# Layer 1's rows inside and behind the attention loop: other step lengths, products in three of four quarters, half steps of differential attention

## The chip, the cores and the metric

The kernel runs on one core of a Trainium2 chip. The metric is device time in microseconds. The kernel before took 1200.21 us (median of three runs, 1198.93 to 1204.29). A profile is of one execution, taken by the hardware profiler; its times are microseconds from the start of its span. Engines are PE (TensorE), DVE (VectorE), ACT (ScalarE), POOL (GpSimd) and SP (SyncE), each with its own queue of instructions.

## The reference

Two transformer blocks on x of shape (8, 512, 128), in float32. `ln` is a layer norm without weights.

```python
xn = ln(x)
x = x + attention_16_heads_causal(xn) + soft_mixture_of_8_experts(xn)      # layer 0
xn = ln(x)
x = x + differential_attention(xn) + block(xn)                             # layer 1

def differential_attention(x):          # per batch, 512 rows, one head of 128
    a1, a2 = softmax(q1 @ k1.T * s), softmax(q2 @ k2.T * s)
    out = (a1 - lam * a2) @ v
    return out / rms(out) * 0.2

def block(h):                           # attention runs over the 8 batches (axis 0), per row of 512
    h2 = h + causal_attention_over_batches(ln1(h)) @ proj.T
    z = ln2(h2)
    return h2 + top2_of_8_experts(z)    # each expert takes at most 1280 of the 8192 choices
```

The attention inside `block` couples, for one row position, the batch s with the batches 0 to s. So its work for batch s grows with n = s + 1, and it needs layer 0's result of the batches up to s only.

## The kernel before, in words

Rows lie on 128 partitions, four row blocks (`NI`) to a batch. The program has these stages.

1. Layer 0's mixture of experts (until about 276 us), with loads beside it.
2. **The attention loop.** It runs over steps e_ from -8 to 99; each has four quarters n, and `slot_ = 4 * e_ + n` numbers them, so the loop ends with slot 399. A step treats a third of one group of four heads of a batch (four groups to a batch, 12 steps to a batch). In each quarter PE makes scores for the exponential pass (`e_head`, L965), whose exponentials ACT takes (L970), and, eight steps ahead, scores for a pass that finds the row maxima (`m_head`, L932), which DVE reduces with a mask (L942). At the end of a step POOL masks the exponentials (`e_mask`, L975), and PE multiplies the masked exponentials of the step before with v (`av`, L989). Every half batch DVE makes `q2` (L952) from the maxima. After four groups, `out_x` (L1026) adds the result to `x_all`, and the batch's lead begins. Within the loop each engine's instructions keep exactly the order in which the program states them (`in_order`).
3. **The leads.** `lead(s)` is a generator that makes layer 1's rows of batch s: layer norm (`ln_stats`, `ln_apply`), transposes and qkv (L566, evacuated by DVE at L573), then products of q and k on POOL (`times`, L585) summed by DVE (`sum_q`, L609), softmax over batches, products with v on POOL (L585 again) summed by DVE (`sum_v`, L639), the projection, the second layer norm, routing (L697 to L761), and eight scatters of rows into the experts' slots in HBM, issued by POOL (L768). Each `yield k, where` says that the lead goes on after k slots at the earliest, and for `"pe"` only in quarter 1, for `"pool"` only in a quarter in which POOL is free for it. `step_leads` is called once a slot and takes each lead one yield further when its time has come; in one slot only one lead gets the `"pool"` grant. Leads also wait for each other's tiles (`after`).
4. **Behind the loop**, `diff([0..5])` computes differential attention of batches 0 to 5. It is a generator too: first qkv, then a first pair of scores, then 24 units (six batches, four row blocks), each with transposes (L161), scores two units ahead (L1138, maxima L1143, exponentials L1148, combination L1161) and the product with v (L1176); a batch's last unit normalises and adds into `x_all` (L1197). After each of its steps, six slots of `step_leads` follow, in each of which POOL is free. When the generator has ended, the slots go on alone until all leads have ended. Here the Tile framework's scheduler may reorder instructions.
5. The eight experts. Each loads its slots (`xe`, L1235) when all scatters of all leads have landed, runs two matrix products (L1263, L1270), and scatters its rows back (L1280).
6. `diff([6, 7])` with `final(b)` between its steps: load of the experts' rows, two additions on DVE (L1298), store.

PSUM tiles of tag `t` are seven in the loop and two behind it. A lead's value product tiles (`prod`) are three.

## Time and profile before

| | |
|---|---|
| runs, us | 1198.93, 1200.21, 1204.29 |
| profiled execution, us | 1204.13 |
| its span, us | 1202.4 |
| mean granted clock of PE | 0.917 |
| busy PE, DVE, ACT, POOL, us | 1017.4, 744.8, 547.9, 426.0 |
| last mask of the loop (L975) ends | 726.2 |
| last `x_all` of batch 5 (L1197) starts | 937.16 |
| first expert matmul (L1263) starts | 986.44 |

Busy times are unions over the span and not additive over engines. In the lists of single instructions the first number is the start in us from the start of the span, the second the length in us; then come engine, line, operation, output and inputs, shapes, and in brackets the idle time of the engine before it with what ended that. In the windows by stage each row is a stretch of the span with the busy time of each engine in it; the number of instructions is in parentheses. In the slices each digit is the busy share of a fortieth of the span in tenths (9 is 90% or more), PEclk the granted clock of PE in tenths.

### The profile page before, as it was taken

Reading aid. Unit: us, or ns where it says so; the run is one execution under the profiler, and the core shown is the slowest. Engines: PE = TensorE matmul, PEld = TensorE weight load, DVE = VectorE, ACT = ScalarE, POOL = GpSimd, SP = SyncE. Lnnn points to the kernel's source line nnn. Section 1 sums busy time; section 2 is a strip of 40 time slices with the busy share of each in tenths; the row PEclk is TensorE's granted clock in tenths of the full one; section 3 lists DMA queues with packets and bytes.
Section 4 is the critical chain, followed back from the end, with each engine's and each line's share of the span. In section 5 each row is a group of like instructions: output and inputs, shape, how many; then the busy total and the mean of one; then the engine's idle time right before and its main releaser. Section 6 shows DMA issues by size and latency. Waiting matters only on the chain. (4 is left out here: it accounts for less than half of the span.)

```text
span 1202.4 us, 19250 instructions
## 1 busy us (share of the span) xinstructions
PE 1017.4 (85%) x6780; PEld 642.4 (53%) x6780; DVE 744.8 (62%) x2622; ACT 547.9 (46%) x1236; POOL 426.0 (35%) x544
## 2 busy tenths in 40 slices
PE   3889989898999999999999996867685329998985
PEld 1457557675555545554555543544544217776753
DVE  6823533587577777877778857869797322222256
ACT  2455436332667656665566454444443102222244
POOL 4500000002144443546274357344444324544420
PEclk9899989997899999999899988789797559999998
DMA  8760000000000000000000004000000022112052
GB/s 232 168 191 1 1 1 1 1 1 1 1 1 2 1 2 1 2 17 4 4 18 1 1 19 140 1 19 0 16 1 10 9 53 66 49 32 73 11 159 71
DMA packets 48689, 41.51 MB, mean 35 GB/s; under 512 B 8747, under 2 KB 42838, under 8 KB 48592
## 3 DMA queue, kind: packets, MB, share of 16 engines
q1 hardware_dynamic: 43168, 33.19, 9.9%
q0 software_dynamic: 4608, 6.69, 1.8%
q8 instruction: 54, 0.88, 0.3%
q10 hardware_dynamic: 816, 0.39, 0.1%
q14 instruction: 43, 0.35, 0.1%
HBM read 21.88 MB, written 21.27 MB: 36 GB/s over the span
## 5 line engine op out<-in xcount | busy, mean ns | idle before, releaser
L942 DVE CUSTOM_DVE_ANT_0 junk<-sm,cmask 128x128 f32<-128x128 f32 (+3 forms) x512 | 227.8, 486 | 87.9 <-PE sm L932 50.2
L970 ACT ACTIVATE pt<-se 128x384 f32<-128x384 f32 (+1 forms) x384 | 183.6, 527 | 147.0 <-PE se L965 94.7
L932 PE MATMUL sm<-kj,qT 32*128 32x128 f32 (+3 forms) x1024 | 234.4, 497 | 7.5 <-DVE mcol L942 4.4
L965 PE MATMUL se<-q,kj 32*128 32x512 f32 (+3 forms) x1024 | 211.8, 483 | 3.8 <-DVE mcol L942 2.6
L975 POOL TENSOR_SCALAR_AFFINE_SELECT pt<-pt 128x512 f32<-128x512 f32 (+1 forms) x96 | 79.1, 824 | 189.1 <-ACT pt L970 188.9
L965 PEld LDWEIGHTS se<-q,kj 32*128 32x128 f32 x1024 | 100.7, 190 | 84.7 <-DVE mcol L942 31.4
L932 PEld LDWEIGHTS sm<-kj,qT 32*128 32x128 f32 x1024 | 113.7, 195 | 22.3 <-DVE mcol L942 9.5
L1280 POOL DMA_INDIRECT yd<-es,to x80 | 77.8, 972 | 99.2 <-DVE es L1276 78.4
L989 PE MATMUL po<-pt,vpad 128*9 128x512 f32 (+3 forms) x1024 | 89.5, 446 | 6.4 <-POOL pt L975 6.4
L1266 ACT ACTIVATE hTm<-phm 128x1024 f32<-128x1024 f32 (+1 forms) x48 | 42.2, 882 | 114.9 <-PE phm L1263 73.4
L1270 PEld LDWEIGHTS pem<-w,hTm 128*128 128x128 f32 x640 | 77.1, 191 | 17.8 <-ACT hTm L1266 11.4
L768 POOL DMA_INDIRECT xs<-l_z,sput x64 | 63.3, 988 | 57.1 <-issue 43.3
L1138 PE MATMUL s<-qk,qk 128*128 128x512 f32 x128 | 68.0, 651 | 18.0 <-ACT ex L1148 14.0
L1263 PE MATMUL phm<-xeT,w 128*128 128x512 f32 (+1 forms) x192 | 76.7, 531 | 7.1 <-DVE xeT L1255 7.1
L1270 PE MATMUL pem<-w,hTm 128*128 128x128 f32 x640 | 81.2, 278 | 1.0 <-ACT hTm L1266 0.7
L1276 DVE TENSOR_SCALAR es<-pem,wt 128x128 f32<-128x128 f32 x80 | 22.9, 345 | 72.4 <-PE pem L1270 66.3
L585 POOL TENSOR_TENSOR l_prod<-l_qkv 128x64 f32<-128x64 f32 (+7 forms) x64 | 50.3, 810 | 33.0 <-DVE l_qkv L573 27.6
L1148 ACT ACTIVATE ex<-s,nm 128x512 f32<-128x512 f32 x64 | 43.6, 688 | 34.6 <-DVE nm L1144 28.3
L585 POOL TENSOR_TENSOR l_prod<-l_qkv,l_sc 128x64 f32<-128x64 f32 (+7 forms) x64 | 43.5, 708 | 43.4 <-ACT l_sc L624 36.6
L809 POOL MEMSET rows<- 128x16 f32 x1 | 0.1, 112 | 160.9 <-PE ph L376 160.9
L1263 PEld LDWEIGHTS phm<-xeT,w 128*128 128x128 f32 x192 | 34.1, 193 | 29.4 <-issue 18.1
L989 PEld LDWEIGHTS po<-pt,vpad 128*9 128x9 f32 x1024 | 18.8, 90 | 54.1 <-issue 27.0
(268 smaller groups left out, 1962.2 us busy)
## 6 DMA issues: line engine op xcount, KB each, us to landing
xs<-cmask SPq DMA_DIRECT2D x1, 5280.0 KB
xe<-xs SPq DMA_DIRECT2D x8, 660.0 KB, 4.6
yd<-cmask SPq DMA_DIRECT2D x1, 4096.0 KB, 35.3
y<-yd SPq DMA_DIRECT2D x8, 512.0 KB, 5.0
x_all<-in_L_attn_x_dram SPq DMA_DIRECT2D x8, 256.0 KB, 6.4
w<-in_L_ffn_w_dram SPq DMA_DIRECT2D x1, 2048.0 KB, 8.8
w<-in_L_ffn_moe_w_dram SPq DMA_DIRECT2D x1, 2048.0 KB, 8.6
out_dram<-x_all SPq DMA_DIRECT2D x8, 256.0 KB, 2.4
```

Source lines behind the costliest of these rows:

```text
L585: nc.gpsimd.tensor_tensor(out=pr[:, :n, :, r], in0=in0, in1=in1(r), op=ALU.mult)
L768: put = nc.gpsimd.indirect_dma_start(out=xs, out_offset=bass.IndirectOffsetOnAxis(ap=sput[:, k, m : m + 1], axis=0), in_=z2[:, i], in_offs ...
L932: nc.tensor.matmul(sc[:, o : o + w], lhsT=st["qT", b][rr, i * P : (i + 1) * P], rhs=st["k", b, j][rr, :w], start=True, stop=True,)
L942: nc.vector.tensor_tensor_reduce(out=junk[:, :w], in0=sc[:, o : o + w], in1=cmask[:, 512 - w : 512], scale=-1.0, scalar=BIG, op0=ALU.add, ...
L965: nc.tensor.matmul(sc[:, o : o + w], lhsT=st["k", b, j][rr, c * P : (c + 1) * P], rhs=st["q2", b, (g % G) // 2][rr, c * P : T], start=True ...
L970: nc.scalar.activation(st["pt", g, k][:, r, :o], sc[:, :o], AF.Exp)
L975: nc.gpsimd.affine_select(out=pt[:, :, :n, :P], in_=pt[:, :, :n, :P], pattern=[[0, 4], [0, n], [1, P]], compare_op=ALU.is_ge, fill=0.0, ba ...
L989: nc.tensor.matmul(po[32 * r : 32 * r + S + 1, c * P : T], lhsT=vpads[b % 3][:, c, 4 * r + j, :], rhs=pt[:, r, o : o + w], start=(c == 0), ...
L1138: nc.tensor.matmul(sc[:, k, :], lhsT=dd["qk", b, 2 * k][:, i * P : (i + 1) * P], rhs=dd["qk", b, 2 * k + 1], start=True, stop=True,)
L1263: nc.tensor.matmul(ph[:, k, :w], lhsT=w1_1[:, e, hc * P : (hc + 1) * P], rhs=xeT[:, :w], start=True, stop=True)
L1270: nc.tensor.matmul(pe[:, k * D : (k + 1) * D], lhsT=hT[:, hc, k * P : (k + 1) * P], rhs=w2_1[:, e, hc, :], start=(hc == 0), stop=(hc == NH ...
L1280: back = nc.gpsimd.indirect_dma_start(out=yd, out_offset=bass.IndirectOffsetOnAxis(ap=to[:, c : c + 1], axis=0), in_=es[:, c], in_offset=N ...
```

## The change

Six places set other slots or another grouping; every operation stays.

- After the reciprocal root in `ln_stats` the lead waits 5 slots, not 6.
- In qkv, the four matmuls are issued together into two PSUM tiles; then, one slot on, the first tile's two evacuations, and another slot on the second's. Before, each half was issued and evacuated in turn, with a wait for quarter 1 between. The wait before the products is 3 slots, not 5.
- In `both`, the sum of the product before shares the slot with the product that follows, where before it had a slot to itself; for n up to 3 it now waits for a POOL quarter (before: two slots).
- In the loop POOL is free for leads in quarters 0, 1 and 2 (before: 1 and 2).
- In `diff`, a second `yield` splits each unit behind its scores.
- Behind the loop four slots, not six, follow each step of `diff`; and the finals are called at the steps that correspond.

```diff
@@ ln_stats
-        yield 6, ""
+        yield 5, ""
@@ lead
+        pqs = []
         for ip in range(NI // 2):
             pq = psum_t(f"pqkv_{s_}_{ip}")
             for k in range(2):
...
-            yield 1, ""
-            for k in range(2):
-                i = 2 * ip + k
-                nc.vector.scalar_tensor_tensor(
...
-            yield (2, "pe") if ip == 0 else (5, "pool")
+            pqs.append(pq)
+        for i in range(NI):
+            if i % 2 == 0:
+                yield 1, ""
+            nc.vector.scalar_tensor_tensor(
...
+        yield 3, "pool"
@@ both
                 yield from times_(i)
                 if i:
                     if n <= 3:
-                        yield 2, ""
+                        yield 1, "pool"
                     sum_(i - 1)
-                    yield 1, "pool"
@@ the loop
-                step_leads(4 * e_ + n, n == 1, n in (1, 2))
+                step_leads(4 * e_ + n, n == 1, n < 3)
@@ diff
                 diff_T(b, i)
                 if m + 2 < len(us):
                     diff_scores(*us[m + 2])
+                yield
                 if i == 1 and bs.index(b) + 1 < len(bs):
                     diff_qkv(bs[bs.index(b) + 1])
                 diff_out(b, i)
@@ behind the loop
-            for n in range(6):
+            for n in range(4):
                 step_leads(slot_, n == 1, True)
                 slot_ += 1
@@ the end
-            if m >= 4:
-                final(m - 4)
+            if m >= 7 and m % 2:
+                final((m - 7) // 2)
```

More of the change, by code (lines that the diff above doesn't have):

```diff
@@ L569, in lead @@
                 )
-            yield 1, ""
-            for k in range(2):
-                i = 2 * ip + k
-                nc.vector.scalar_tensor_tensor(
-                    out=qkv[:, s_, i].rearrange("p v c s -> p (v c s)"), in0=pq[:, k * 256 : (k + 1) * 256],
-                    scalar=r2[:, i : i + 1], in1=l1p["bias"][:, : 2 * D], op0=ALU.mult, op1=ALU.add,
-                )
-            yield (2, "pe") if ip == 0 else (5, "pool")
+            pqs.append(pq)
[3 more added lines that the diff above has]
+            nc.vector.scalar_tensor_tensor(
+                out=qkv[:, s_, i].rearrange("p v c s -> p (v c s)"),
+                in0=pqs[i // 2][:, (i % 2) * 256 : (i % 2 + 1) * 256],
+                scalar=r2[:, i : i + 1], in1=l1p["bias"][:, : 2 * D], op0=ALU.mult, op1=ALU.add,
+            )
+        yield 3, "pool"
         yield from after("sc", s_ - 1)
```

## The prediction

> **What bounds the kernel now.** I read the page's forty slices first (30 us each).

> ```profile
> PE   3889989898999999999999996867685329998985
> DVE  6823533587577777877778857869797322222256
> PEclk9899989997899999999899988789797559999998
> ```

> PE is the limit in slices 9 to 23 (the attention loop) and 33 to 38 (the experts). Between them it is not, and in slices 30 to 32 it hardly works. The windows by stage give the sizes (stretch, length, busy PE, PEld, DVE, ACT, POOL, clock, DMA share, GB/s):

> ```profile
> 525.00:620.00 95.00, 90.88 (x732) 50.87 (x730) 72.12 (x315) 55.77 (x128) 50.86 (x72) 0.93 0.04 13
> 620.00:730.00 110.00, 101.89 (x896) 55.74 (x894) 79.99 (x325) 64.72 (x138) 58.27 (x75) 0.97 0.03 9
> ...
> 790.00:850.00 60.00, 42.32 (x188) 26.53 (x186) 50.74 (x139) 25.91 (x72) 23.00 (x23) 0.89 0.01 4
> ...
> 910.00:945.00 35.00, 19.02 (x96) 15.99 (x96) 23.86 (x107) 11.37 (x36) 14.41 (x14) 0.65 0.03 9
> 945.00:984.00 39.00, 4.54 (x16) 3.44 (x16) 6.60 (x35) 2.46 (x6) 15.96 (x16) 0.50 0.13 36
> ```

> Behind the loop DVE is the busiest engine (85%), and from 945 none is. DVE's timeline says why:

> ```profile
> 937.16 1.12 DVE L1197 SCALAR_TENSOR_TENSOR x_all<-po,ri,x_all 128x128 f32<-128x128 f32 x4
> ...
> 953.73 1.23 DVE L520 SCALAR_TENSOR_TENSOR nmr_l<-mv_l,rs_l 128x4 f32<-128x4 f32 x1 [9.07 <-POOL rs_l L127]
> ...
> 966.88 0.17 DVE L761 TENSOR_SCALAR sput<-r_hq 128x8 uint32<-128x8 f32 x1
> 984.40 0.17 DVE L1240 TENSOR_SCALAR first<-xe 128x10 f32<-128x10 f32 x1 [17.35 <-DMA xe<-xs]
> ```

> Differential attention of batches 0 to 5 is over at 938. What follows is the last lead alone: it waits 9.07 us because its reciprocal root stands on POOL behind eight scatters of the lead before, its own slots are known at 967, eight scatters and one load later (984) the experts start. POOL's timeline shows the queue:

> ```profile
> 951.65 0.97 POOL L768 DMA_INDIRECT xs<-l_z,sput  x1 [0.30 <-issue]
> 952.63 1.07 POOL L127 TENSOR_TENSOR rs_l<-ve_l,mhalf 128x4 f32<-128x4 f32 x1
> ```

> So 46 us (938 to 984) are a latency chain, and the 190 us before are DVE's. In the loop a mark per half batch (L952) shows what leads cost there:

> ```profile
> 347.60 0.69 DVE L952 TENSOR_TENSOR q<-mT,qT 128x512 f32<-128x512 f32 x1
> 371.31 0.69 DVE L952 TENSOR_TENSOR q<-mT,qT 128x512 f32<-128x512 f32 x1
> ...
> 501.31 0.69 DVE L952 TENSOR_TENSOR q<-mT,qT 128x512 f32<-128x512 f32 x1
> 534.57 0.69 DVE L952 TENSOR_TENSOR q<-mT,qT 128x512 f32<-128x512 f32 x1
> ```

> 23.7 us without a lead, 33.3 us with 11 us of lead work on DVE.

> [...] `ex` (L1161) takes 883 ns behind the loop, beside POOL's products, and 745 ns at the end, where POOL does nothing.

> **The change, part by part.** All edits set slots, none removes arithmetic. The attention loop ends with slot 399. I walked every lead's yields through the slots in both versions. Last scatters, leads 0 to 7: before 218, 274, 362, 436, 484, 532, 580, 628; after 190, 246, 294, 346, 394, 440, 488, 532. The differential attention spans slots 400 to 555 before (26 steps of 6) and 400 to 599 after (50 of 4). So the lead-only tail of 73 slots goes; the last lead ends after 33 of 50 half steps, with two batches of work still ahead.

> (1) *What leaves the stretch behind the loop.* Lead prices on DVE, summed from the rows by shape: routing 7.8 us (39.1 us in five leads), second layer norm 3.0, first 3.1, qkv 1.9; for lead 4 q sums 3.3, softmax 2.4, value sums 5.8; for lead 7 4.8, 3.2, 8.5. At slot 400 before, there remain lead 3's routing and a little (8.5), lead 4 from its last two sums (20.6), 5 from qkv (25.8), 6 (28.5) and 7 (32.2): 116 us. After: lead 5's rest (9.5), 6 from its sums (25.6), 7 (32.2): 67 us. The differential attention adds 98 us to both (29.1 nm, 21.2 ex, 9.5 cc, 6.7 x_all, 31 smaller).

> Before, from the first row maximum (747.5) to 938, 98 + 116 - 18 (done before) - 14 (left after) = 182 us of such durations took 190.5 us: 1.05 per us (durations overlap a little, so that holds idle time too). After: in the changed program's order on DVE all of lead 6's sums stand ahead of the first row maximum. So from the last mask on: eight scatters 8 x 1.28 = 10.2; seven products at 1.12, x_all 1.27, rs_l 1.0: 10.1; sum, maximum, subtract, exp 1.08 + 0.89 + 0.62 + 0.58 = 3.2; eight products at 1.0 and rs_x: 9.0; last sum, scaling, v copy 3.2. That is 36 us against 21 before (last mask ends 726.2). Then 98 + 67 - 19 = 146 us at 1.05 = 153, less 3, as the experts' first matmul stands ahead of the last four x_all updates: 186 us from last mask to first expert matmul (L1263), against 986.4 - 726.2 = 260. Minus 74 us. Inside it I leave standing two new waits: lead 7's second sum behind lead 5's scatters (some 10 us), and nmr_l of lead 7 behind lead 6's (some 9), like those that 1.05 already holds.

> (2) *What enters the loop.* By half batches, the leads put 79 us of DVE work under the loop's masked sums before, 109 after. The fifteen half batches took 706.2 - 299.5 = 406.7 us, 51 above 15 x 23.7: 0.65 us per us of lead work, PE's part and clock dips included. 30 more cost 19. The other 19 us of moved DVE work fall in the last twelve steps, where L942 is over and DVE is at 12.6 of 30 us (700 to 730): only their PE work counts, some 7 us, half of it covered: 3. On POOL 28 products (0.7 to 1.1 us) and eight scatters more precede the last mask; with three grants in a step of 4.4 us the mask (0.68 to 1.1) stays within it except in scatters (3 x 1.28 + 0.85 = 4.7), and `av` asks for the mask a step later: nothing, else up to 35 us (below). Plus 22 us.

> (3) *Two PSUM tiles at once for qkv* (of seven in the loop, two behind it): the tile is freed 1 us later; nothing in the loop, up to 3 us for lead 7, which shares two tiles with the differential attention. *Waits 6 to 5 and 5 to 3, sums in the product's step*: if a product is late, DVE waits in order behind it; inside the 0.65.

> (4) *The experts and the end* (216 us) keep their instructions. The half step leaves each final where it was; DVE's order at the end shifts by a few: within 2 us either way.

> Sum: -74 + 22 = -52. The profiled execution, 1202.4 span and 1204.13 in all, becomes 1150 and 1152; it lay 4 us above the median 1200.21, to which I apply the difference: 1148. About 0.5% (6 us) is what a measurement of this kernel can tell from no change.

> **Rivals.** *DVE becomes the limit of the loop* (dearer): the 30 us cost 1.5 each, as leads now come without pauses and each stall lowers the clock (0.86 in 565 to 602, a half batch of 36.7 us with 11.6 us of leads). +45 +3: 1174. For it: 0.93 in 525 to 620; against it: 24.1 us with as much lead work at 652 to 676. *The loop hides them* (better): 5 us in the loop, since DVE idles a quarter of it, and contention behind it falls (ex and cc back to 745 and 213 ns: 8 us): 1200 - 82 + 8 = 1126. *Slower*: POOL's third grant delays the masks, PE waits in order for `pt`, and its gaps cut its clock. Its place is the loop from 421 to 706, ten half batches of 28.5 us on average now. The waits alone are at most 28 products and eight scatters at 0.97, some 35 us, and leave 1183 (1148 + 35); it decides where all ten cost 36 us each, as the slowest seen did (36.7). At 38 us: 10 x 9.5 = 95, so 1200 - 74 + 95 = 1221. Against it: PE waits for `pt` 6.4 us in 421 us. *The change does nothing behind the loop*, because DVE's new waits (10 and 9) and the later first maximum eat the gain: 205 rather than 186: 1167; it shares the dearer range.

> **How the numbers follow.** Likeliest 0.58 (1148, own range 1136 to 1160); dearer, by either cause, 0.22 (to 1178); better 0.15 (to 1118); slower or level 0.05, of which slower 0.03, same 0.02. The range 1118 to 1178 leaves out the last and the ends.

> **What would show it.** Last x_all update of batch 5 close before the first L1263 matmul, no clock of 0.5 there; last mask near 748, first matmul near 934; the lead's last scatter some 50 us earlier than that. Half batches at 28 to 33 us from 421 on. I am wrong if the loop grows by more than 50 us, or if PE waits long for `pt`, or DVE's share behind the loop falls under 75%.

## The result and the profile after

The changed kernel takes 1192.72 us (median), the kernel before 1199.26 us beside it: a ratio of 0.9944, with a 95% interval of 0.992 to 0.9968. It is faster, by 6.5 us (0.6%) and not by 52, and 1192.72 lies outside the predicted range of 1118 to 1178. The profiled execution of the changed kernel took 1192.14 us, its span 1190.2 at a mean clock of 0.907 (before: 1202.4 at 0.917). The spans differ by 12.2 us, more than the medians, since the profiled execution of before lay 5 us above its median.

After the change the line numbers shift by two or three: the masked maxima are L944, `q2` L954, the masks L977, the sums L611 and L641, the row maxima of the differential attention L1145, the experts' first matmul L1266. The page's slices of the changed kernel (PE, DVE and the granted clock; slices are 29.8 us):

```profile
PE   3889989898999999998998988956675989999995
DVE  6823532486677787878687888538695853322256
PEclk9899989997899999898896989567987989999998
```

The nearly empty slices 30 to 32 of before (counted from 0, as in the prediction) are gone, as intended. But in slices 21, 25 and 26, in the attention loop and at its end (625 to 655 and 744 to 803 us; the last mask ends at 786.1), the clock has fallen to 0.6, 0.5 and 0.6.

To see sizes I cut both executions at the same events: the DVE `q2` near 397 us, the last `q2` (the end of the part that makes masked maxima, called the masked part below), the last mask, the first expert matmul, the end. The stretch from the last `q2` to the last mask is called the last steps: it runs from quarter 1 of step 89 to the end of step 95. The columns of the windows are stretch, length, busy PE, PEld, DVE, ACT, POOL, clock, DMA share, GB/s. The kernel before:

```profile
396.30:706.20 309.90, 297.81 (x2528) 169.30 (x2526) 244.94 (x1047) 187.16 (x414) 147.84 (x223) 0.96 0.02 6
706.20:726.20 20.00, 16.88 (x164) 7.48 (x164) 5.69 (x10) 13.49 (x30) 14.76 (x17) 1.00 0.05 15
726.20:986.40 260.20, 160.65 (x684) 104.59 (x684) 187.85 (x573) 92.33 (x247) 113.88 (x114) 0.78 0.10 29
986.40:1202.40 216.00, 191.75 (x1064) 137.35 (x1064) 77.01 (x236) 67.95 (x114) 77.76 (x80) 0.97 0.22 64
```

The changed kernel, cut at the same events:

```profile
398.40:744.10 345.70, 319.00 (x2584) 181.48 (x2580) 278.51 (x1129) 191.92 (x430) 185.17 (x261) 0.90 0.02 8
744.10:786.10 42.00, 41.27 (x168) 18.95 (x168) 22.63 (x63) 17.25 (x40) 15.75 (x18) 0.50 0.00 1
786.10:980.60 194.50, 133.92 (x610) 83.93 (x608) 134.16 (x426) 80.58 (x214) 75.11 (x71) 0.85 0.12 35
980.60:1190.20 209.60, 190.81 (x1070) 137.46 (x1068) 80.02 (x247) 69.57 (x122) 77.87 (x80) 0.98 0.23 66
```

Behind the loop 65.7 us are won (260.2 to 194.5) and 6.4 more behind that. The loop pays most of it back: 2 us ahead of the first mark, 35.8 in the masked part, 22.0 in its last steps, 60 in all, against a forecast of 22. Those last steps took twice as long with PE busy for 98% of them: at clock 0.50 throughout, where before it was 1.00.

Where the loop's time went can be counted. In the masked part PE idled 12.1 us before (length less busy PE in the rows above) and 26.7 after. From windows of 4 us, adding 2 x (1 - clock) x length, PE was at half clock for 27.4 us before and for 66.0 after. As an estimate, let half of the time at half clock be lost: 14.6 us more idle time and 38.6 / 2 are 33.9 of the 35.8 us. The same matmuls became longer, as the page's groups show, first before, then after (columns: line, engine, operation, output and inputs, count, busy us, mean ns, idle before):

```profile
L965 PE MATMUL se<-q,kj 32*128 32x512 f32 (+3 forms) x1024 | 211.8, 483 | 3.8 <-DVE mcol L942 2.6
```

```profile
L967 PE MATMUL se<-q,kj 32*128 32x512 f32 (+3 forms) x1024 | 229.4, 517 | 6.0 <-DVE q L954 3.0
```

How a half batch loses 18 us is seen in the marks of the changed kernel (start, length, engine, line), and in windows of 4 us within the longest:

```profile
579.68 0.68 DVE L954 TENSOR_TENSOR q<-mT,qT 128x512 f32<-128x512 f32 x1
606.84 0.69 DVE L954 TENSOR_TENSOR q<-mT,qT 128x512 f32<-128x512 f32 x1
648.33 0.68 DVE L954 TENSOR_TENSOR q<-mT,qT 128x512 f32<-128x512 f32 x1
```

```profile
614.00:618.00 4.00, 3.80 (x36) 1.93 (x28) 3.90 (x14) 3.92 (x10) 0.68 (x1) 1.00 0.01 2
618.00:622.00 4.00, 3.44 (x33) 2.30 (x26) 3.83 (x16) 2.07 (x6) 1.05 (x2) 1.00 0.02 4
622.00:626.00 4.00, 4.00 (x27) 2.38 (x28) 3.76 (x15) 0.59 (x2) 3.75 (x8) 0.68 0.00 0
626.00:630.00 4.00, 4.00 (x30) 2.43 (x28) 3.76 (x16) 2.35 (x5) 3.75 (x8) 0.50 0.00 0
...
638.00:642.00 4.00, 4.00 (x21) 1.69 (x20) 0.63 (x3) 0.85 (x2) 0.00 (x0) 0.69 0.00 0
```

DVE is full from 614 on (3.76 to 3.90 of 4). PE, which needs its maxima and its PSUM tiles freed, idles 0.2 and then 0.56 us, and from about 623 its clock is halved. Now PE is late, and at 638 DVE has little to do (0.63 of 4). A lead's routing (L697 to L763, small DVE instructions, several in each slot) stands in each of the four half batches above 34 us (34.2, 39.7, 41.5, 35.1); so the next theory was that its density, not the sum of lead work, is what costs.

### The profile page after: what moved, and what is told of

Same layout as the page of the kernel before. It is cut to its first block, busy times and chain, and to the rows that moved or that the text cites. A ratio compares the mean times of both kernels' runs of the same rounds, so it can differ in the third digit from the quotient of the medians.

```text
span 1190.2 us, 19219 instructions
## 1 busy us (share of the span) xinstructions
PE 1036.3 (87%) x6780; PEld 646.5 (54%) x6780; DVE 745.9 (63%) x2622; ACT 546.7 (46%) x1236; POOL 426.4 (36%) x544
## 3 DMA queue, kind: packets, MB, share of 16 engines
q1 hardware_dynamic: 43168, 33.19, 10.1%
## 4 chain that ended last, share of the span: by engine, by line
PE 48%; DVE 15%; issue 5%; POOL 4%; ACT 4%; DMA 1%; POOLq 0%; SPq 0%; DVEq 0%; ACTq 0%
PE se L967 9%; PE pem L1273 6%; PE sm L934 6%; PE phm L1266 5%; PE po L991 5%; PE s L1140 3%; DVE junk L944 3%; PE pqk L1125 2%; POOL xs L770 2%; PE pq L858 2%; PE po L1178 1%; PE ot L161 1%; POOL l_prod L588 1%; PE pqkv L567 1%; DVE l_at L641 1%
## 5 line engine op out<-in xcount | busy, mean ns | idle before, releaser
L944 DVE CUSTOM_DVE_ANT_0 junk<-sm,cmask 128x128 f32<-128x128 f32 (+3 forms) x512 | 228.7, 486 | 91.1 <-PE sm L934 55.2
L934 PE MATMUL sm<-kj,qT 32*128 32x256 f32 (+3 forms) x1024 | 246.4, 511 | 9.3 <-DVE mcol L944 5.6
L967 PE MATMUL se<-q,kj 32*128 32x512 f32 (+3 forms) x1024 | 229.4, 517 | 6.0 <-DVE q L954 3.0
L967 PEld LDWEIGHTS se<-q,kj 32*128 32x128 f32 x1024 | 108.2, 203 | 93.2 <-DVE mcol L944 26.5
L977 POOL TENSOR_SCALAR_AFFINE_SELECT pt<-pt 128x512 f32<-128x512 f32 (+1 forms) x96 | 79.0, 823 | 202.1 <-ACT pt L972 199.6
L934 PEld LDWEIGHTS sm<-kj,qT 32*128 32x128 f32 x1024 | 118.4, 202 | 26.1 <-DVE mcol L944 11.5
L991 PE MATMUL po<-pt,vpad 128*9 128x512 f32 (+3 forms) x1024 | 97.2, 478 | 3.1 <-POOL pt L977 3.1
L1266 PE MATMUL phm<-xeT,w 128*128 128x512 f32 (+1 forms) x192 | 75.0, 524 | 3.1 <-DVE xeT L1258 2.3
L1150 ACT ACTIVATE ex<-s,nm 128x512 f32<-128x512 f32 x64 | 43.6, 690 | 32.8 <-DVE nm L1146 29.6
L1266 PEld LDWEIGHTS phm<-xeT,w 128*128 128x128 f32 x192 | 33.8, 190 | 24.7 <-issue 17.9
```

The lines of the kernel that those rows point to most:

```text
L934: nc.tensor.matmul(sc[:, o : o + w], lhsT=st["qT", b][rr, i * P : (i + 1) * P], rhs=st["k", b, j][rr, :w], start=True, stop=True,)
L944: nc.vector.tensor_tensor_reduce(out=junk[:, :w], in0=sc[:, o : o + w], in1=cmask[:, 512 - w : 512], scale=-1.0, scalar=BIG, op0=ALU.add, ...
L967: nc.tensor.matmul(sc[:, o : o + w], lhsT=st["k", b, j][rr, c * P : (c + 1) * P], rhs=st["q2", b, (g % G) // 2][rr, c * P : T], start=True ...
L977: nc.gpsimd.affine_select(out=pt[:, :, :n, :P], in_=pt[:, :, :n, :P], pattern=[[0, 4], [0, n], [1, P]], compare_op=ALU.is_ge, fill=0.0, ba ...
L991: nc.tensor.matmul(po[32 * r : 32 * r + S + 1, c * P : T], lhsT=vpads[b % 3][:, c, 4 * r + j, :], rhs=pt[:, r, o : o + w], start=(c == 0), ...
L1266: nc.tensor.matmul(ph[:, k, :w], lhsT=w1_1[:, e, hc * P : (hc + 1) * P], rhs=xeT[:, :w], start=True, stop=True)
```

## The runs, by stage

Stages as above: the masked part with PE's idle and half-clock time in it, the last steps to the last mask, from there to the first expert matmul, the experts and the end. Each median has the ratio to the kernel before that was timed beside it; stages are of the one profiled execution. All in us. The small differences between stages need care: four kernels have the loop of before (before, warm_before, tail_only, tail6), and their masked parts took 304.0 to 309.9 us; four have the loop of the change (the change, warm_after, loop_only, warm_loop), and theirs took 340.4 to 351.0.

| run | median | ratio, 95% interval | masked part (idle, half clock) | to last mask | to experts | end |
|---|---|---|---|---|---|---|
| before | 1199.26 | | 309.9 (12.1, 27.4) | 20.0 | 260.2 | 216.0 |
| the change | 1192.72 | 0.9944 (0.992 to 0.9968) | 345.7 (26.7, 66.0) | 42.0 | 194.5 | 209.6 |
| warm_after | 1184.79 | 0.9887 (0.9836 to 0.9937) | 351.0 (25.9, 75.1) | 34.7 | 194.1 | 209.5 |
| warm_before | 1203.56 | 1.0041 (1.0023 to 1.0059) | 309.8 (12.1, 27.4) | 22.8 | 257.2 | 219.0 |
| grants2 | 1174.69 | 0.9803 (0.9749 to 0.9856) | 321.2 (22.3, 34.2) | 26.3 | 219.5 | 209.7 |
| tail_only | 1194.82 | 0.9959 (0.9936 to 0.9982) | 309.9 (12.0, 27.4) | 20.0 | 251.7 | 217.7 |
| tail6 | 1201.80 | 1.0015 (0.9997 to 1.0032) | 304.0 (11.7, 17.0) | 20.0 | 263.7 | 209.7 |
| loop_only | 1176.11 | 0.9779 (0.9749 to 0.981) | 340.4 (28.1, 53.6) | 41.4 | 180.4 | 211.7 |
| g2_loop | 1169.64 | 0.9729 (0.9697 to 0.9762) | 318.9 (18.0, 41.0) | 25.4 | 206.6 | 218.3 |
| pool_small | 1142.68 | 0.9504 (0.9477 to 0.9532) | 332.5 (20.0, 47.8) | 25.1 | 174.9 | 209.3 |
| dve_small | 1182.46 | 0.9838 (0.9807 to 0.987) | 339.0 (24.0, 55.4) | 42.0 | 188.6 | 209.5 |
| warm_loop | 1171.27 | 0.9753 (0.9727 to 0.9778) | 342.4 (27.5, 55.9) | 35.8 | 180.6 | 211.6 |
| spread_loop | 1162.63 | 0.9696 (0.9655 to 0.9738) | 310.6 (9.9, 27.4) | 33.5 | 202.5 | 218.1 |
| spread_warm | 1157.55 | 0.9649 (0.962 to 0.9677) | 311.9 (10.2, 27.4) | 28.6 | 200.8 | 215.9 |
| spread_before | 1189.81 | 0.9896 (0.9832 to 0.9959) | 300.9 (11.7, 20.5) | 28.2 | 247.6 | 217.9 |
| spread_after | 1168.10 | 0.9753 (0.9706 to 0.98) | 314.1 (14.0, 23.9) | 32.0 | 212.5 | 209.2 |
| half_spread_warm | 1148.03 | 0.9577 (0.953 to 0.9624) | 320.0 (15.6, 34.1) | 24.9 | 196.8 | 209.6 |

## Experiments: the parts of the change

**The third grant alone taken back (grants2).**

```diff
-                step_leads(4 * e_ + n, n == 1, n < 3)
+                step_leads(4 * e_ + n, n == 1, n in (1, 2))
```

> The changed kernel with one edit undone: the leads get POOL's grant in two of four quarters, as before. Seven products and six scatters more than in the kernel before precede the last mask, instead of 28 and eight; the last lead ends at slot 568 of 599. Theory A (the density of lead work in the loop costs clock): the last mask moves from 786 to 735 to 750, from there to the first expert matmul 225 to 235 us instead of 194.5, time 1170 to 1182. Theory B (each us of lead work on DVE costs the same wherever it stands, so moving it back gains nothing): last mask near 745, behind it 235 to 245, time 1190 to 1196.

It came as theory A said: 1174.69 us, the last mask at 743.7. The masked part pays back 24.5 of its 35.8 us, the last steps 15.7 of 22, and the stretch behind the loop gets 25 us longer (219.5, somewhat less than the 225 to 235 expected). So most of the loop's cost hangs on the third grant, which admits 97 products in place of 76 ahead of the last mask.

**The half steps alone (tail_only), and with six slots in each (tail6).** Edits of the kernel before; tail6 leaves the six slots as they are:

```diff
                 if m + 2 < len(us):
                     diff_scores(*us[m + 2])
+                yield
...
-            for n in range(6):
+            for n in range(4):
...
-            if m >= 4:
-                final(m - 4)
+            if m >= 7 and m % 2:
+                final((m - 7) // 2)
```

> The kernel before with only the half steps of the differential attention (yield in the middle of a step, four slots in a step, the last outputs at the same places); the loop is that of before. The last mask stays at 726 +-3. The last lead ends at slot 628, 29 slots behind the last half step at 599, instead of 73. Theory A (the gain behind the loop comes from covering the lead's latency chain, 46 us, and not from moved work): 260 falls to 225 to 240 us, time 1170 to 1185. Theory B (without moved work the lead still stands alone at the end): 250 to 262 us, time 1192 to 1200.

> The kernel before with the half steps and six slots in each, so that the leads, which still end at slot 628, end ahead of the differential attention's last half step (slot 699); the loop is that of before. Theory A (lead work costs the same under the loop as behind it, and what is won is the cover of the last lead's latency): last mask at 726, first expert matmul 225 to 235 us later, against 260 before and 252 with four slots; time 1165 to 1176. Theory B (the work has to be moved into the loop for a gain): 250 to 260 us, time 1190 to 1200.

Theory B both times: 252 us and 264 us behind the loop, times of 1194.82 and 1201.80 (those of tail6 a little above its ranges). In tail6 the last scatter came 241 us behind the last mask instead of 251, but the attention now ended last (its last `x_all` at 990.1, behind the first expert matmul), and DVE was busy for 180.5 of 263.7 us. Putting attention over the last lead's chain did not bring the experts forward. That the two strands wait for each other on DVE is the likely reason; it was not tried by itself.

**The loop's edits alone (loop_only).** The changed kernel with the diff of tail_only undone.

> The changed kernel with the differential attention and the end as before: whole steps, six slots in each; the third grant, the shorter waits and the qkv pair stay. Theory A (the half steps do little by themselves): loop as in the changed kernel, last mask 780 to 790, from there to the first expert matmul 195 to 205 us, time 1194 to 1202. Theory B (the half steps are what takes the lead off the end): 215 us or more, time 1210 or more.

Neither theory: 1176.11 us. Without the half steps the stretch behind the loop is 180.4 us and not 194.5. So the two parts of the change do not add up: the half steps alone gain 5 us (1194.82 against 1200.08), the loop's edits alone 25 (1176.11 against 1200.91), both together 6.5. Two stretches, from 60 and from 100 us behind the last mask, show where they differ, first in the changed kernel, then in loop_only (columns as before):

```profile
846.10:866.10 20.00, 7.79 (x42) 5.37 (x43) 11.66 (x22) 4.23 (x15) 15.13 (x15) 0.82 0.04 13
886.10:906.10 20.00, 4.58 (x22) 4.08 (x21) 18.84 (x69) 3.86 (x11) 3.01 (x3) 0.59 0.00 0
```

```profile
842.00:862.00 20.00, 15.65 (x70) 10.48 (x69) 18.65 (x53) 9.77 (x27) 12.53 (x12) 0.83 0.02 7
882.00:902.00 20.00, 16.36 (x87) 10.36 (x86) 19.41 (x89) 10.70 (x31) 0.10 (x1) 1.00 0.00 1
```

Two half steps of four slots give the leads eight slots per unit of attention, a whole step gives them six. In the changed kernel leads 6 and 7 stand in the queues with little attention between them; PE has 4.58 us of work in 20, and the attention is left over: the last scatter comes 164 us behind the last mask (loop_only: 169), but the last `x_all` of the attention 199 us (loop_only: 184). DVE's work behind the loop is the same, 134.2 and 132.7 us. That the eight slots are the cause is argued: half steps of three slots, which would keep six to a unit, were not run.

**Whole steps and two grants (g2_loop).** loop_only with the edit of grants2.

> The loop's edits without the third grant, with whole steps of six slots; the last lead ends at slot 568, the last step at 555. Theory A (whole steps serve the stretch behind the loop better, as 180 against 194 us showed with the third grant): masked-sum part 321 us, last mask 744, first expert matmul 205 to 215 us later, time 1160 to 1170. Theory B (half steps are better where the leads end late): 220 to 232 us, time 1175 to 1187.

Theory A: 1169.64 us and 206.6 behind the loop, against 219.5 with half steps. Again whole steps are better there, by 13 us; at the experts 8.6 of these are given back (218.3 against 209.7), and the medians differ by 5 us, with intervals that overlap.

## Experiments: what the leads cost in the loop

**Small products, small sums (pool_small, dve_small).** Edits of the changed kernel. In pool_small `times` forms one product (first pair of lines) and both sums read it n times, as a broadcast. In dve_small `sum_q` reads 4 of 8 elements (second pair) and `sum_v` the first batch's product alone.

```diff
-                    out=pr[:, :n, :, r], in0=in0, in1=in1(r), op=ALU.mult
+                    out=pr[:, :1, :, r], in0=in0[:, :1], in1=in1(r)[:, :1], op=ALU.mult
...
-                in_=prods["q", i][:, :n].rearrange("p t v r s -> p (t v r) s"), axis=AX.X, op=ALU.add,
+                in_=prods["q", i][:, :n].rearrange("p t v r s -> p (t v r) s")[:, :, :4], axis=AX.X, op=ALU.add,
...
```

> The changed kernel with POOL's products of the leads made small: each forms the product with the first batch only, and the sums read that one product again in place of the others (as many elements for DVE; the sums are of other numbers). Of some 52 us of products on POOL in the masked-sum part of the loop about 12 remain; DVE keeps its 109 us of lead work. That part (the DVE q at 398 us to the last at 744) took 345.7 us, and 309.9 in the kernel before. Theory A (DVE, in order, is what the added lead work costs): 335 to 346 us. Theory B (POOL's products, which hold DVE and delay the masks, are what it costs): 310 to 325 us.

> The changed kernel with the leads' sums on DVE made small: those of the scores read half of each head, those of the values the first batch alone (other numbers come out); POOL's products stay. Some 18 of 109 us of lead work on DVE are gone in the masked-sum part of the loop, 345.7 us long in the changed kernel and 309.9 in the one before (79 us of lead work). Theory A (DVE): the part falls to 320 to 330 us. Theory B (POOL's products): 338 to 346 us.

The masked part took 332.5 us with small products, between the two theories, and 339.0 with small sums, in the range of theory B. By the trace pool_small took 25 us of lead work off POOL in that part (97.9 to 72.8) for 13.2 us of time (and DVE's own lead instructions took 12 us less), dve_small 11.6 off DVE (121.0 to 109.4) for 6.7. The 6.7 are within what kernels with this loop differ by (339.0 beside 340.4 to 351.0), so a price per us cannot be taken from them. Neither comes near the 36 us; the long half batches stayed (39.5 and 38.6 in pool_small, 38.7 and 40.6 in dve_small, 39.7 and 41.5 in the changed kernel). So neither products nor sums are most of what makes these long. pool_small did something else, though: its last steps took 25.1 us, at full clock (below).

**The routing spread out (spread_loop, spread_after, spread_before).** In leads 0 to 3, a yield behind each DVE instruction of the routing that had none, in loop_only, in the changed kernel and in the kernel before. No instruction is added or removed.

```diff
         nc.vector.tensor_reduce(out=r1, in_=pb, axis=AX.X, op=ALU.add)
+        if s_ < 4:
+            yield 1, ""
         nc.vector.reciprocal(r1, r1)
+        if s_ < 4:
+            yield 1, ""
...
```

> The run with the loop's edits and whole steps of six slots (1176 us; masked-sum part 340.4 us, then 41.4 us to the last mask), with one thing changed: in leads 0 to 3 a yield of one slot follows every DVE instruction of the routing, so that the same 7.8 us of small DVE instructions come over some 35 slots instead of 8. Theory A (what the leads cost in the loop is DVE saturated in the bursts of the routing, the PE gaps and half clock that follow): the half batches of 39.7, 40.5 and 34.7 us fall to 28 to 32, the part to 310 to 325 us, time 1145 to 1162. Theory B (the amount of lead work counts, not how dense it comes): part 335 to 345 us, time 1172 to 1182.

> The changed kernel itself with a yield after each DVE instruction of the routing of leads 0 to 3. Theory A (bursts): the masked-sum part falls from 345.7 to 310 to 320 us, the stretch from there to the last mask from 42 to 25 to 36, behind it 200 to 215 us instead of 194.5; time 1165 to 1180. Theory B (the bursts cost this only with whole steps): 335 us or more, time 1188 or more.

> The kernel before with the same yields. Theory A (its long half batches of 33.3, 30.5, 36.7 and 30.1 us are the routings of its three leads in the loop): none is above 31, the part of 309.9 us falls to 288 to 300 us; the leads end later behind the loop, so the time is 1188 to 1205. Theory B: the part stays within 5 us of 310.

In loop_only the masked part falls from 340.4 to 310.6 us, in the changed kernel from 345.7 to 314.1: theory A in both. The changed kernel's time falls to 1168.10 us from 1192.72; that of loop_only to 1162.63, just outside the range, since its stretch behind the loop grows from 180.4 to 202.5. PE's idle time there halves (26.7 to 14.0) and its half-clock time falls from 66.0 to 23.9 us; 12.7 + 42.1 / 2 = 33.8 against 31.6 measured. The marks of the changed kernel with the spread routing, for the same half batches:

```profile
558.16 0.68 DVE L1004 TENSOR_TENSOR q<-mT,qT 128x512 f32<-128x512 f32 x1
586.92 0.68 DVE L1004 TENSOR_TENSOR q<-mT,qT 128x512 f32<-128x512 f32 x1
615.53 0.69 DVE L1004 TENSOR_TENSOR q<-mT,qT 128x512 f32<-128x512 f32 x1
```

28.8 and 28.6 us where 27.2 and 41.5 stood. The half batch behind them grew, from 29.2 to 35.4 us (in spread_loop from 27.5 to 34.3), as lead work now falls there, and the one of 39.7 fell to 27.4. Not all of the gain is density. The spread leads come later, and 10 us of their DVE work (121.0 to 110.8) left the part; at the dearest price that the masked part shows, 35.8 / 38.3 = 0.93 us per us (below), that is 9.5 us. At least some 22 of the 31.6 remain for the density, as an estimate. Spreading also moves the leads against POOL's masks and products; that was not varied apart.

In the kernel before, the four long half batches of 33.3, 30.5, 36.7 and 30.1 us became 27.4, 29.6, 29.4 and 23.2, but two between them grew, from 23.2 to 30.7 and from 27.0 to 29.6. The part fell by 9 to 300.9 us, just above what A allowed and 3 us under the lowest of the four kernels with that loop. That the price per us of lead work taken from that kernel held the bursts of three routings is thus likely and not settled.

## Experiments: the last steps

Why the clock fell at the end of the masked part and stayed down: the timelines of DVE and of POOL in the changed kernel, and PE's next wait.

```profile
738.86 4.33 DVE L511 TENSOR_SCALAR ve_x<-mv_x 128x4 f32<-128x4 f32 x1
743.10 0.15 DVE L520 SCALAR_TENSOR_TENSOR nmr_l<-mv_l,rs_l 128x4 f32<-128x4 f32 x1
743.17 0.94 DVE L611 TENSOR_REDUCE l_sc<-l_prod 128x96 f32<-128x768 f32 x1
...
744.10 0.68 DVE L954 TENSOR_TENSOR q<-mT,qT 128x512 f32<-128x512 f32 x1
```

```profile
736.51 2.88 POOL L588 TENSOR_TENSOR l_prod<-l_qkv 128x384 f32<-128x384 f32 x3
739.36 1.25 POOL L671 TENSOR_TENSOR x_all<-x_all,l_ha 128x512 f32<-128x512 f32 x1
740.57 0.67 POOL L977 TENSOR_SCALAR_AFFINE_SELECT pt<-pt 128x512 f32<-128x512 f32 x1
741.23 1.92 POOL L588 TENSOR_TENSOR l_prod<-l_qkv 128x384 f32<-128x384 f32 x2
```

```profile
744.83 2.08 PE L967 MATMUL se<-q,kj 32*128 32x512 f32 x4 [2.70 <-DVE q L954]
```

An addition on 128 x 4 numbers lasts 4.33 us and ends within 0.05 us of the end of POOL's unbroken row (741.23 + 1.92 = 743.15). Behind it, in order, stands the last `q2`, and PE waits 2.70 us for it; within that wait, at 742.9, the clock falls from 1.00 to 0.50. The same instruction took 4.33 us in loop_only, 4.73 in dve_small, 4.35 in warm_after and 4.34 in warm_loop, and in all four, too, it ended within 0.05 us of POOL's last product. In pool_small POOL makes the same row of seven in 3.3 us and not 6.6, from 726.43 to 729.72, and the addition took 0.98 us; in grants2 and g2_loop it took 1.41 and 1.39. In these three it also ended 0.03 us behind the last instruction of POOL's row. So it lasts until POOL's row ends, and where the row ends sooner behind its start, it is shorter. That POOL's instructions hold it is argued from these ends; by what means, the traces do not show.

How much of the longer last steps is the clock's, pool_small shows. Without the long addition it entered them at full clock, and it has the same 168 matmuls there as the changed kernel, shape for shape (columns as in the windows above):

```profile
730.80:755.70 24.90, 22.56 (x168) 11.31 (x168) 19.03 (x61) 17.40 (x40) 10.35 (x18) 1.00 0.00 1
```

That is 25.1 us between the two events against 42.0, so some 17 of the 22 us follow the clock (POOL's products were smaller, too: 10.35 us busy against 15.75). In dve_small DVE was busy for 17.0 us there against 22.6, and the stretch still took 42.0 us at 0.50: DVE does not set its length.

**Matmuls added to the last steps (warm_after, warm_before, warm_loop).** `warm` issues one matmul of qT with k, on the 32 partitions that the score product would have, into a PSUM tile of tag `t`; the bases are the changed kernel, the kernel before and loop_only.

```diff
                 if m_ < N3:
                     m_head(gm, km, (n + 2) % 4)
+                elif e_ < N3:
+                    warm(ge, ke, (n + 2) % 4)
```

> The changed kernel, with 32 more matmuls in the last eight whole steps of the loop, in which the masked sums have ended: one in each quarter, of the shape that the score product of the first layer has there, on another row group, into a PSUM tile that nobody reads. Theory A (the loop grew because a stall at 740 us left PE at half clock, and the matmuls that remain there cannot bring it back): the clock in the stretch from the last DVE q to the last mask is 0.85 or more instead of 0.50, the stretch falls from 42 us to 25 to 29, and the time falls by 10 to 16 us, to 1177 to 1183. Theory B (the stretch is long because DVE or POOL paces it, the clock only follows): the clock stays low or the stretch stays 38 us or more, and the time is 1190 to 1200.

> Control of the former: the same 32 matmuls, with a result that nobody reads, in the kernel before. There the clock is 1.00 in that stretch, so theory A expects nothing to win: 1197 to 1204. If it becomes faster by over 5 us, the added matmuls do something other than keep the clock.

> The same base with the 32 matmuls of the earlier run in the last eight steps (a PSUM tile that nobody reads). Theory A (half clock is most of the 41.4 us between the last DVE q and the last mask, and matmuls beside them bring the clock back): 26 to 35 us, time 1162 to 1172. Theory B: no change beyond 4 us.

The stretch of warm_after (columns as in the windows above):

```profile
750.60:785.20 34.60, 27.95 (x216) 14.97 (x216) 23.89 (x62) 17.60 (x41) 15.65 (x18) 0.85 0.00 1
```

With the added matmuls (216 records for 168) the clock is 0.85 instead of 0.50, and the stretch falls from 42.0 to 34.7 us; in warm_loop from 41.4 to 35.8. That the matmuls bring the clock back is shown. The gain is half of what A said. PE is idle for 6.7 us in the stretch, and two thirds of that are one wait:

```profile
776.35 0.76 PE L976 MATMUL se<-q,kj 32*128 32x256 f32 x1 [4.46 <-DVE att L1020]
```

`att` stands on DVE behind a lead's routing (771.15 to 774.4) and a sum, and with this wait the clock is halved a second time: it is 1.00 from 754.6 to 775.1 and 0.50 for the next 6.8 us. In warm_loop the wait is 4.45 us. So a burst of routing costs here, too. In time, the intervals of warm_after and of the change overlap (up to 0.9937, from 0.992), as do those of warm_loop and loop_only, so that a gain of 5 to 8 us is likely and not settled. In the kernel before, where the clock was 1.00, the added matmuls cost 0.4%.

**Both, and a lighter spread (spread_warm, half_spread_warm).** The base is loop_only with the added matmuls. The second has a yield behind every other one of these instructions.

> Both of these together. If the spread by itself keeps the clock up at the end of the loop, the added matmuls do nothing more: within 5 us of the spread alone. If the end still falls into half clock: 8 to 15 us less than the spread alone.

> The run with the spread and the added matmuls (1157.6 us), with a yield after every second of those DVE instructions only. If the stretch behind the loop grew from 180 to 201 us because the leads end later, it is 185 to 193 us here; if the masked-sum part needs the whole spread, it is 318 to 330 us instead of 312. Time 1148 to 1162; a gain of less than 3 us would mean that the one gives back what the other takes.

With the whole spread the added matmuls take 5 us off the last steps (33.5 to 28.6); the medians differ by as much, with intervals that overlap. The lighter spread, 12 yields for 25, has the part at 320.0 us (318 to 330 was expected), the stretch behind the loop at 196.8 (185 to 193), the last steps at 24.9 with the clock at 0.99, and a median of 1148.03 us: 4.2% faster than the kernel before (interval 3.8 to 4.7) and the best version found that computes the same (pool_small, at 1142.68, does not). The stretch behind the loop lies above what the later leads explained, so that reading of it is not confirmed.

## Why the prediction was wrong

**Step 2, "Plus 22 us", failed: it was 60.** Its price, 0.65 us per us of lead work on DVE, was an average over the kernel before, used as if it were a constant. It failed in two ways.

- In the masked part 19 us were forecast and 35.8 came. The added DVE work was 38 us (82.7 to 121.0 by durations), not 30; some 9 us of that are instructions that lasted longer than the median of their form (16.2 us in the part, 7.0 before). And the price was 35.8 / 38.3 = 0.93. With the routing spread in both kernels, 22 us more lead work (89.0 to 110.8) cost 13.2, some 0.6 per us; kernels with one loop differ by 6 to 11 us in this part, so that figure is rough. The forecast's 0.65 thus fits work that comes evenly. Denser leads fill DVE for 10 to 20 us at a time, PE idles (0.6 to 2.8 us in the 4 us ahead of each of the ten falls of the clock in the changed kernel's masked part), and the halved clock (66.0 us in that part) does the rest.
- For the last twelve steps of the loop (88 to 99) 3 us were forecast, as only PE's part of the moved work would count, and 22.0 came between the last `q2` and the last mask. Some 17 of them go with the clock: pool_small, with the same matmuls, took 25.1 us at 1.00 and not 42.0 at 0.50. I had priced the work that falls there, and not in which clock PE would enter.

**The rival "DVE becomes the limit of the loop" (1174) was the right mechanism**, stalls that lower the clock (ten falls to 0.50 in the masked part of the changed kernel), though not each does: PE idled for 1.31 us from 482.4 to 486.4 and for 1.01 from 586.4 to 590.4, at a clock of 1.00 throughout. It put 45 us on the masked part, which had 35.8, and 3 on the last steps, which had 22.0. The point held against it was a misreading. The half batch from 652 to 676 in the kernel before, 24.1 us long, does not have as much lead work as that of 36.7 us from 565 on: by durations it has 6.5 us and the other 15.5, and DVE is busy for 20.5 and 28.8 us in them. The long one holds a whole routing, the short one a single instruction of one. Two of the signs named for a wrong forecast are what happened: a loop that grows by more than 50 us, and a DVE share behind the loop under 75% (134.2 of 194.5 us, 69%). The forecast of the last mask (748) missed by 38 us. Half batches of 28 to 33 us were forecast; 34.2, 39.7, 41.5 and 35.1 lie above.

**The rival "slower" had the wrong place.** PE waited 3.8 us for the masks in the masked part before and 3.1 after: POOL's third grant does not make PE wait longer for them. It hurts by what it lets in: denser leads on DVE, and the row of products at 737 to 743 us.

**Step 1 was nearly right: -65.7 against -74.** The stretch to the first row maximum was 36.6 us (forecast 36). The rest was 158 us and not 150. The forecast took DVE as the limit there at 1.05 us per us of work; DVE was busy for 134 of the 194.5 us, so that it often waited. Its cause was misjudged as well: the prediction put the end of the lead-only tail down to both parts of the change together, and loop_only shows that the loop's edits do it alone, 80 us, and that the half steps take 14 of these back. The rival "does nothing behind the loop", with 205 us, has 8.5 of its 19 us.

**Step 3** (PSUM tiles) held: PE waited once for a tile of the qkv pair, 1.9 us. **Step 4** (within 2 us) was short by 4: the experts and the end took 6.4 us less, 5.5 of which are PE idle time. Ten of the seventeen profiled executions have 209 to 212 us there, the others 216 to 219, and the traces show what goes with it. In all ten the attention of batch 5 ends last: its last `x_all` starts 2 to 5 us behind the first expert matmul, which comes 10 to 29 us behind the last scatter. In all seven others the attention had ended before, and the first expert matmul follows the last scatter by 8.6 to 8.8 us. So the change gained here by letting the attention, and not the last lead, end last; it was not varied by itself.

The sum of the profiled spans closes: 59.9 - 65.7 - 6.4 = -12.2.

## What to carry to other kernels

The lead work moved under this loop, with PE busy for 96% of the masked part before, had no constant price: some 0.6 us per us where the routing was spread, 0.93 where bursts kept DVE busy for 3.76 to 3.90 of 4 us (from 614 to 630) and PE went idle waiting for it. So price such work per burst, against the free time in that stretch, look at what the granted clock does behind every gap, and look at whether the phase that comes next brings the clock back (in the last steps here it did not). Two edits that each gain should be tried apart: here they took from each other.
